# Two-layer attention kernel: the next batch's input and left operand fetched as 4 KB rows, three of seven operand parts fetched later

## The chip, the cores and the metric

One core of a Trainium2 chip runs the whole program. The metric is device time in microseconds (us) of one execution; the median of repeated runs is compared. Engines are named as in the profile: PE (TensorE matmul), PEld (its weight loads), DVE (VectorE), ACT (ScalarE), POOL (GpSimd), SP (SyncE, which here only issues DMAs). SPq is SP's instruction queue.

## The reference

Input x is (8, 512, 32, 32) float32: eight batches b, C = 512 channels, T = 1024 tokens. Two residual layers run in sequence, each on a group-normalised input:

```
x = x + layer0(gn(x))
x = x + layer1(gn(x))

layer 0: group norm again, q,k,v = qkv_w . n, 8 heads of 64, softmax(q k) v,
         out = proj_w . (xf + a) + proj_b
layer 1: q = w_q . x, k = w_k . x, v = w_v . x          (8 heads of 64)
         attn = einsum('bhqd,bhdT->bhqT', q, k) * scale
         attn = einsum('gh,bhqT->bgqT', w_head, attn)   # heads are mixed
         attn = softmax(attn), then instance norm over each (b, head)
         out  = attn v, then w_proj, + b_proj
```

The change touches layer 1 alone.

## The kernel before

**Stages.** Layer 0 runs over the eight batches first and writes its result to DRAM tensors `x1_d[b]`. Layer 1 then runs over the eight batches (loop L1930). For a batch it has three tensors in SBUF: `q`, `k` and `v`, each 128 partitions wide. The attention of a batch (class `Attention1`, L1620) is cut into eight tiles p of 128 queries, and the order of instructions on every engine is written out by hand, in `step(p, t, ag)` (L1854) with p from 0 to 8 and t from 0 to 3. Four sub-steps t make one step p; a step works on tile p (scores), on tile p-1 (head mixing and exponentials) and on tile p-2 (products with v). An `Agenda` object holds extra work by slot number 4p + t; `ag.at(slot, fn)` adds a function to a slot and `step` runs it there.

**The path of one tile.** `scores` (L1628) multiplies q and k for all eight heads, for 512 keys at a time (kh = 0 or 1), and ACT copies the result from PSUM to a `raw` tile (128 x 8 x 512; two buffers in all, so one for each kh). The head mixing needs the heads on different partitions. So `regroup` (L1649) moves the raw tile through the DMA engines: for each of four slices s and two halves r one DMA from 16 source partitions to a slot of `re`, 128 partitions x 512 floats, 256 KB. This makes 16 DMAs or 4 MB per step, all issued by SP (L1653). `mix` (L1663, matmul L1672) multiplies a slot of `re` by `wmix`; it needs both key halves of its slice. The first mix of tile p, `mix(p, 0)`, is issued in step p + 1 at t = 0, after the scores 0 to 2 and part of the value products.

**The order on SP's queue.** In each step SP issues six regroups (kh 0, s = 0, 1, 2) at t = 1, two more (kh 0, s = 3) at t = 2, then the prefetch pieces of that step if there are any (`self.piece`, L1918 and L1919), and at t = 3 the eight regroups of kh 1. A DMA waits on the completion of the DMA eight places earlier on the queue, because eight semaphores are used in turn.

**The prefetch.** During the attention of batch b the operands of batch b + 1 are loaded. `a.pieces` (L1942 and L1943) is a list of 30 DMAs of 128 KB, each 128 partitions x 256 floats (1 KB): sixteen of `y_piece` (L1337), which fill the next normalised input `y` (4 channel blocks of 128 x 1024) from `x1_d`, and fourteen of `left_piece` (L1302), which fill the next left operand for k. Four are issued in each of the steps 1 to 4, five in steps 5 and 6 and four in step 7. So steps 1 to 4 carry y and steps 5 to 7 carry the left operand. In the last batch (L1964) there is no next batch; eight pieces of w_proj (`p_piece`, L1327) are issued in steps 1 and 2, four in each, and nothing later.

**The left operand.** Projections use a scheme of seven products on 2 x 2 blocks (class `Projection`, L1363). The left operand has seven parts, each 128 x 512 floats. Product m reads the part given in `products` (L1374):

```
1: (0, self.b11), 2: (1, self.b21), 3: (6, self.b22), 4: (2, self.t[:, 3]),
5: (3, self.t[:, 0]), 6: (4, self.t[:, 1]), 7: (5, self.t[:, 2]),
```

**The tail.** Step 8 has no scores; it is called the tail below, with what follows it. There the k projection of batch b + 1 is woven in: products 1, 2, 6, 7 at slots 4 NT - 0.5, + 0.5, + 1.5 and + 2.5 (NT = 8), product 5 after `a.sums(last)` (L1981), products 4 and 3 later still (L1990). At slot 4 NT + 1 `left_p` (L1426) loads the 1792 KB left operand of the output projection into a raw buffer; SP then issues the next wv (L1325), the reciprocals of the last tile (L1779, L1786), the residual rows (L1515), the left operand for q (L1317) and the outputs (L1535).

Of the kernel before, what the change touches and what calls it, by code (L numbers as in the profile page):

```python
# [18 lines left out]
P = 128  # L19
# [448 lines left out]
def tile_two_attention_layers(  # L468
# [19 lines left out]
    nc = tc.nc  # L488
    B, C, T = x_d.shape
    H = w_head.shape[0]  # L490
    D = C // H
    NCC = C // P
    NT = T // P
# [9 lines left out]
    x1_d = [dram.tile([C, T], F32, tag=f"x1_{b}", name=f"x1_{b}") for b in range(B)]  # L503
# [193 lines left out]
    with ExitStack() as l0:  # L697
# [21 lines left out]
        for c in range(NCC):  # L719
# [5 lines left out]
        HC = C // 2  # L725
# [4 lines left out]
        left_d = {  # L730
            which: dram.tile([P, 7 * 2 * HC], F32, tag=f"left_{which}", name=f"left_{which}")
            for which in SOURCES
        }
        left_t = {}

        def left_tile(which, b):
            t = wpool.tile([P, 7, 2, HC], F32, tag="left", name=f"left_{which}_{b}")
            left_t[which] = t
            return t
# [463 lines left out]
        for b in range(B):  # L1203
            more = b + 1 < B
            ag = Agenda()
# [61 lines left out]
    with ExitStack() as l1:  # L1267
# [21 lines left out]
        y_t, qo_t, k_t, v_t = ({0: t["1"]} for t in (n_t, q_t, k_t, v_t))  # L1289
        w_t = {}  # L1290
# [3 lines left out]
        HC = C // 2  # L1294
# [4 lines left out]
                [P, 7, 2 * HC], F32, tag="left", name=f"left_{key[0]}_{key[1]}"  # L1299
            )  # L1300

        def left_piece(key, i):  # L1302

            if i == 0:
                left_tile(key)
            f, h = i // 2, i % 2
            return nc.sync.dma_start(
                out=w_t[key][:, f, ts(h, HC)],
                in_=left_d[key[0] + "1"][:, (2 * f + h) * HC : (2 * f + h + 1) * HC],
            )  # L1310

        def load_left(key, t=None):
# [11 lines left out]
            for c in range(NCC):  # L1324
                nc.sync.dma_start(out=w_t[key][:, c], in_=src[ts(c, P)])  # L1325

        def p_piece(i):  # L1327

            if i == 0:
                left_tile(("p", B - 1))  # L1330
                w_t["p", B - 1] = w_t["p", B - 1][:, :NCC]
            c, h = i // 2, i % 2
            return nc.sync.dma_start(
                out=w_t["p", B - 1][:, c, ts(h, HC)], in_=w_projT[ts(c, P), ts(h, HC)]
            )

        def y_piece(b, i):  # L1337

            if i == 0:
                y_t[b] = shared.tile([P, NCC, T], F32, tag="n", name=f"y_{b}")  # L1340
            c, r = i // 4, i % 4
            return nc.sync.dma_start(
                out=y_t[b][:, c, ts(r, HC)], in_=x1_d[b][ts(c, P), ts(r, HC)]
            )

        def normalize1(b, c):
            normalize_to(y_t[b][:, c], b, c)
# [272 lines left out]
        class Attention1:  # L1620
# [233 lines left out]
            def step(self, p, t, ag):  # L1854

                new, old, older = p < NT, p >= 1, p >= 2
                if t == 0:
                    if new:
                        for i in range(3):
                            self.scores(p, i)  # L1860
                    if older:
                        self.values(p - 2, 0, 2, 3)
                        self.leave(p - 2, 0)
                        self.sums(p - 2)
                        if p % 2 == 0 and p >= 4:
                            self.divide(p // 2 - 2, nc.gpsimd)
                    if old:
                        self.mix(p - 1, 0)()
                    ag.run(4 * p - 0.5)
                elif t == 1:  # L1870
                    if older:
                        self.values(p - 2, 1, 0)
                        self.flip(p - 1, 0)
                        self.totals(p - 2)
                        self.moments(p - 1, 0)
                    if new:
                        self.scores(p, 3)
                    if old:
                        self.mix(p - 1, 1)()
                    ag.run(4 * p + 0.5)  # L1880
                elif t == 2:
                    if older:
                        self.values(p - 2, 1, 1)
                    if new:
                        self.scores(p, 4)
                        self.scores(p, 5)
                    if old and not new:
                        self.mix(p - 1, 2)()
                    ag.run(4 * p + 1.5)
                    if older:  # L1890
                        self.values(p - 2, 1, 2, 3)
                        self.leave(p - 2, 1)
                    if old and new:
                        self.mix(p - 1, 2)()
                else:
                    if new:
                        self.scores(p, 6)
                        if old:
                            self.values(p - 1, 0, 0)
                            second = self.mix(p - 1, 3)  # L1900
                        self.scores(p, 7)
                        if old:
                            second()
                            self.values(p - 1, 0, 1)
                    else:
                        self.mix(p - 1, 3)()
                        self.values(p - 1, 0, 0, 1)
                    ag.run(4 * p + 2.5)
                k_leave()
                if p == 1 or old and t:  # L1910
                    self.flip(p - 1, t)
                    self.moments(p - 1, t)
                if new:
                    for kh, s in (
                        (), ((0, 0), (0, 1), (0, 2)), ((0, 3),), ((1, 0), (1, 1), (1, 2), (1, 3)),
                    )[t]:
                        self.regroup(p, kh, s)
                if old and t == 2:  # L1918
                    self.piece(4 if p < 5 else 5)  # L1919
                ag.run(4 * p + t)  # L1920

        def load_wv(b):
# [7 lines left out]
        for b in range(B):  # L1930
            more = b + 1 < B
            a = Attention1(b)
            ag = Agenda()
            for i in range(NV):
                ag.at(1 + 2 * i, lambda i=i: v_pair(b, NV + i))
            if b == 0:
                stages = group_stages(B - 1, B, small_psum1)
                for i in range(3):
                    ag.at(i, stages[i])
                ag.at(3, v_sums)  # L1940
            if more:
                a.pieces += [lambda i=i: y_piece(b + 1, i) for i in range(4 * NCC)]  # L1942
                a.pieces += [lambda i=i: left_piece(("k", b + 1), i) for i in range(14)]  # L1943
                for c in range(NCC):
                    ag.at(20 + c, lambda c=c: normalize1(b + 1, c))

                def k_go(*ms):
                    if not kp:
                        kp.append(k_projection(b + 1))
                    for m in ms:  # L1950
                        kp[0].products(m)
                        due.append(lambda m=m: kp[0].leave(m))

                kp = []
                ag.at(4 * NT - 0.5, lambda: right_tile(b + 1))
                ag.at(4 * NT - 0.5, lambda: k_go(1))
                ag.at(4 * NT, lambda: right_y(b + 1, [0, 1]))
                ag.at(4 * NT + 0.5, lambda: k_go(2))
                ag.at(4 * NT + 1, lambda: right_y(b + 1, [2, 3]))
                ag.at(4 * NT + 1, lambda: left_p(b))  # L1960
                ag.at(4 * NT + 1.5, lambda: k_go(6))
                ag.at(4 * NT + 2.5, lambda: k_go(7))
            else:
                a.pieces += [lambda i=i: p_piece(i) for i in range(2 * NCC)]  # L1964
            for p in range(NT + 1):
                for t in range(4):
                    a.step(p, t, ag)
            ag.flush()
            k_leave()
            last = NT - 1  # L1970
            a.sums(last)
            if not more:
                a.values(last, 0, 2, 3)
                a.leave(last, 0)
                a.values(last, 1, 0, 1, 2, 3)
                a.leave(last, 1)
                a.totals(last)
                a.instance()
                out1_last(a)
                continue  # L1980
            k_go(5)  # L1981
            a.values(last, 0, 2, 3)
            a.leave(last, 0)
            load_wv(b + 1)
            a.values(last, 1, 0, 1, 2, 3)
            a.leave(last, 1)
            a.totals(last)
            a.instance()
            k_leave()
            k_go(4, 3)  # L1990
            k_leave()
            a.instance_end()
            v_pair(b + 1, 0)
            a.divide(NCH - 1)
            for g in range(H):
                a.affine(g)
            right_o = re_t[:, 4:8]
            combine_right(right_o, out_view(b))
            op = out1(b, right_o)
            load_left(("q", b + 1))  # L2000
            v_pair(b + 1, 1)
            a.check()
            op.run()
            q_projection(b + 1).run()
# [70 lines left out]
```

## Time and profile before

| what | value |
|---|---|
| runs shown | 4078.61, 4088.58, 4091.99 us; median 4088.58 |
| profiled execution, its own time | 4076.99 us |
| span of its profile | 4075.2 us |
| mean granted PE clock | 0.991 |
| busy share of the span | PE 96%, PEld 45%, DVE 70%, ACT 48%, POOL 3% |
| layer 1 | from 1800 us on, eight batches |
| DMA share in layer 1 | 0.61 to 0.69 of 16 engines by stages of 275 to 400 us, 0.23 to 0.25 in layer 0 |
| regroup DMAs | 1024, 256 KB each |
| y pieces, left pieces | 112 and 98, 128 KB each |

The page gives busy time by engine, then 40 slices of the span, the DMA queues, and groups of instructions by source line with the idle time ahead of them and what ended it. A timeline row is: start, duration, engine, line, operation, output <- inputs, count, and in brackets the idle time before it and what released it. A windows row gives, for a stretch, the engines' busy time, the granted PE clock as a share of full speed, the busy share of the DMA engines and the GB/s that they moved. Busy shares of DMA can exceed 1, because the records of packets overlap.

### The profile page before, as it was taken

Reading aid. Unit: us, or ns where it says so; the run is one execution under the profiler, and the core shown is the slowest. Engines: PE = TensorE matmul, PEld = TensorE weight load, DVE = VectorE, ACT = ScalarE, POOL = GpSimd, SP = SyncE. Lnnn points to the kernel's source line nnn. Section 1 sums busy time; section 2 is a strip of 40 time slices with the busy share of each in tenths; the row PEclk is TensorE's granted clock in tenths of the full one; section 3 lists DMA queues with packets and bytes.
Section 4 is the critical chain, followed back from the end, with each engine's and each line's share of the span. In section 5 each row is a group of like instructions: output and inputs, shape, how many; then the busy total and the mean of one; then the engine's idle time right before and its main releaser. Section 6 shows DMA issues by size and latency. Waiting matters only on the chain. (4 is left out here: it accounts for less than half of the span.)

```text
span 4075.2 us, 96122 instructions
## 1 busy us (share of the span) xinstructions
PE 3906.7 (96%) x41932; PEld 1839.3 (45%) x41932; DVE 2835.6 (70%) x4124; ACT 1967.2 (48%) x2431; POOL 128.6 (3%) x150
## 2 busy tenths in 40 slices
PE   8999999999999999999999999999999999999997
PEld 4353535353434434344535545445444444445354
DVE  4748474757666665748859859759679578488597
ACT  1717263635445453517427437347157175174274
POOL 0000000000000000000000000001000000000000
PEclk9999999999999999999999999999999999999999
DMA  3313131212112111238639549468378287386384
GB/s 127 109 47 115 50 115 45 89 47 79 46 60 71 65 54 59 74 104 213 172 118 226 173 123 228 136 154 224 119 183 224 84 217 184 114 214 180 115 214 126
DMA packets 268637, 519.13 MB, mean 127 GB/s; under 512 B 49840, under 2 KB 84912, under 8 KB 261552
## 3 DMA queue, kind: packets, MB, share of 16 engines
q1 hardware_dynamic: 261664, 497.96, 42.8%
q0 software_dynamic: 6544, 14.94, 1.7%
q8 instruction: 332, 5.44, 0.6%
q14 instruction: 97, 0.79, 0.1%
HBM read 197.16 MB, written 46.92 MB: 60 GB/s over the span
## 5 line engine op out<-in xcount | busy, mean ns | idle before, releaser
L1700 DVE STREAM_TRANSPOSE et<-e 128x2048 f32<-128x2048 f32 x256 | 587.3, 2294 | 153.4 <-ACT e L1685 146.8
L1727 PEld LDWEIGHTS a<-et,v 128*64 128x64 f32 x16384 | 514.3, 140 | 296.7 <-issue 226.9
L1711 DVE BATCH_NORM_STATS2 bn<-e 128x6 f32<-128x512 f32 x1024 | 633.9, 674 | 0.0
L1685 ACT ACTIVATE e<-m 128x1024 f32<-128x1024 f32 x512 | 502.9, 1023 | 237.5 <-issue 134.1
L1089 ACT ACTIVATE e<-s 128x1024 f32<-128x1024 f32 x512 | 497.2, 1026 | 233.8 <-PE s L1084 232.7
L1727 PE MATMUL a<-et,v 128*64 128x64 f32 x16384 | 562.8, 226 | 11.0 <-DVE et L1700 10.4
L1647 ACT COPY raw<-s 128x1024 f32<-128x1024 f32 x480 | 469.8, 1017 | 195.8 <-PE s L1635 165.9
L1097 DVE TENSOR_TENSOR zacc<-zacc,e 128x1024 f32<-128x1024 f32 x384 | 468.7, 1221 | 91.0 <-ACT e L1089 69.0
L1635 PE MATMUL s<-k,q 64*64 64x512 f32 x4096 | 515.9, 607 | 6.2 <-DVE q L1500 3.1
L1084 PE MATMUL s<-q,k 64*64 64x512 f32 x4096 | 490.1, 593 | 2.3 <-ACT e L1089 2.3
L1110 PE MATMUL a<-e,v 64*64 64x512 f32 x4096 | 484.1, 589 | 0.0
L1672 PE MATMUL m<-re,wmix 32*32 32x512 f32 x8192 | 329.3, 617 | 104.7 <-DMA re<-raw 54.7
L1110 PEld LDWEIGHTS a<-e,v 64*64 64x64 f32 x4096 | 156.7, 133 | 282.8 <-issue 282.2
L1084 PEld LDWEIGHTS s<-q,k 64*64 64x64 f32 x4096 | 147.9, 133 | 275.1 <-issue 240.5
L1635 PEld LDWEIGHTS s<-k,q 64*64 64x64 f32 x4096 | 128.4, 132 | 262.5 <-issue 93.6
L1461 PE MATMUL pv<-wv,y 128*128 128x512 f32 x480 | 212.1, 597 | 0.0
L1743 ACT COPY q<-a 64x256 f32<-64x256 f32 x256 | 93.9, 367 | 180.8 <-PE a L1727 178.8
L1672 PEld LDWEIGHTS m<-re,wmix 32*32 32x32 f32 x8192 | 73.6, 103 | 196.6 <-issue 77.8
L1779 POOL DMA_DIRECT2D zd<-rz x56 | 34.6, 619 | 3514.0 <-DVE r L1791 3514.0
L1461 PEld LDWEIGHTS pv<-wv,y 128*128 128x128 f32 x480 | 89.3, 190 | 116.9 <-issue 110.3
L1465 ACT COPY v<-pv 128x512 f32<-128x512 f32 x30 | 17.6, 586 | 218.6 <-PE pv L1461 218.6
L1095 DVE TENSOR_TENSOR zacc<-e,e 128x1024 f32<-128x1024 f32 x64 | 78.3, 1223 | 57.2 <-ACT e L1089 57.2
(315 smaller groups left out, 3951.2 us busy)
## 6 DMA issues: line engine op xcount, KB each, us to landing
re<-raw SPq DMA_DIRECT2D x1024, 256.0 KB
left_q<-left_q SPq DMA_DIRECT2D x17, 1792.0 KB
left_p<-left_p SPq DMA_DIRECT2D x17, 1792.0 KB
left_k<-left_k SPq DMA_DIRECT2D x10, 1792.0 KB
x<-in_x_dram SPq DMA_DIRECT2D x32, 512.0 KB
rzb<-zd SPq DMA_DIRECT2D x128, 128.0 KB
x<-x SPq DMA_DIRECT2D x64, 256.0 KB
left_v<-left_v SPq DMA_DIRECT2D x8, 1792.0 KB
```

The lines of the kernel that those rows point to most:

```text
L1084: nc.tensor.matmul(ps[c * D : c * D + D, m], k[r, hp, k0 : k0 + D], q[r, hp, ts(f, FB)], start=True, stop=True,)
L1089: nc.scalar.activation(e[i], ps, AF.Exp, scale=S0 * S0)
L1097: nc.vector.tensor_add(zacc[g], zacc[g], e[i])
L1110: nc.tensor.matmul(acc[g][a][m * D : m * D + D], v[rows, kc, ts(2 * hp + m, D)], e[i][rows, m], start=(kc == 0), stop=(kc == NG - 1),)
L1461: nc.tensor.matmul(ps[:, m], y_t[b][:, c, ts(2 * i + m, P)], w[:, c], start=(c == 0), stop=(c == NCC - 1),)
L1635: nc.tensor.matmul(ps[c * D : c * D + D, m], qo_t[b][r, p, hp, ts(c, D)], k_t[b][r, hp, ts(kh, FB)], start=True, stop=True,)
L1647: nc.scalar.copy(dst, ps)
L1672: nc.tensor.matmul(ps[a // 2][c * 32 : c * 32 + 32, a % 2].rearrange("p (r h k) -> p h r k", r=2, h=2), wmix[rows].rearrange("p g i -> p ( ...
L1685: nc.scalar.activation(e[:, :, 2 * h : 2 * h + 2].rearrange("p r a k -> p a r k"), ps[h].rearrange("p a (r k) -> p a r k", r=2), AF.Exp,)
L1700: nc.vector.transpose(self.et[p, u].rearrange("p kb (r st a) g q -> p st kb r (a g q)", r=2, st=2)[:, st], self.e[p, s].rearrange("p r a ( ...
L1711: nc.vector.bn_stats(self.bn[p][:, s, a], e[:, :, a].rearrange("p r k -> p k r"))
L1727: nc.tensor.matmul(acc[two * D : two * D + D, s].rearrange("p (x q) -> p x q", q=4), v_t[b][:, kb, ts(g, D)], et[:, kb, :, g], start=(kb = ...
```

## The change

The 30 pieces per batch become eight DMAs. `y_piece` loads one channel block of 128 x 1024 floats (512 KB, 4 KB on each partition) in one DMA. `left_piece(key, f, n)` loads n whole parts in one DMA (4 KB on each partition for n = 2). `self.piece()` issues one entry of the list in each step, so steps 1 to 4 carry one y block each, step 5 the parts 0 and 1, step 6 the parts 4 and 5. The parts 2 and 3 (512 KB) and 6 (256 KB) leave the list; they are put on the agenda at slot 4 NT, at the end of t = 0 of step 8, ahead of `right_y` and of `left_p`. In the last batch `p_piece` loads one block of 256 KB (2 KB on each partition) in each of the steps 1 to 4.

```diff
-        def left_piece(key, i):
+        def left_piece(key, f, n):
-            if i == 0:
+            if f == 0:
                 left_tile(key)
-            f, h = i // 2, i % 2
-            return nc.sync.dma_start(
-                out=w_t[key][:, f, ts(h, HC)],
-                in_=left_d[key[0] + "1"][:, (2 * f + h) * HC : (2 * f + h + 1) * HC],
+            nc.sync.dma_start(
+                out=w_t[key][:, f : f + n].rearrange("p f o -> p (f o)"),
+                in_=left_d[key[0] + "1"][:, 2 * f * HC : 2 * (f + n) * HC],
             )
...
-        def p_piece(i):
+        def p_piece(c):
-            if i == 0:
+            if c == 0:
                 left_tile(("p", B - 1))
                 w_t["p", B - 1] = w_t["p", B - 1][:, :NCC]
-            c, h = i // 2, i % 2
-            return nc.sync.dma_start(
-                out=w_t["p", B - 1][:, c, ts(h, HC)], in_=w_projT[ts(c, P), ts(h, HC)]
-            )
+            nc.sync.dma_start(out=w_t["p", B - 1][:, c], in_=w_projT[ts(c, P)])
-        def y_piece(b, i):
+        def y_piece(b, c):
-            if i == 0:
+            if c == 0:
                 y_t[b] = shared.tile([P, NCC, T], F32, tag="n", name=f"y_{b}")
-            c, r = i // 4, i % 4
-            return nc.sync.dma_start(
-                out=y_t[b][:, c, ts(r, HC)], in_=x1_d[b][ts(c, P), ts(r, HC)]
-            )
+            nc.sync.dma_start(out=y_t[b][:, c], in_=x1_d[b][ts(c, P), :])
...
                 if old and t == 2:
-                    self.piece(4 if p < 5 else 5)
+                    self.piece()
...
-                a.pieces += [lambda i=i: y_piece(b + 1, i) for i in range(4 * NCC)]
-                a.pieces += [lambda i=i: left_piece(("k", b + 1), i) for i in range(14)]
+                a.pieces += [lambda c=c: y_piece(b + 1, c) for c in range(NCC)]
+                a.pieces += [lambda f=f: left_piece(("k", b + 1), f, 2) for f in (0, 4)]
+                ag.at(4 * NT, lambda: left_piece(("k", b + 1), 2, 2))
+                ag.at(4 * NT, lambda: left_piece(("k", b + 1), 6, 1))
...
-                a.pieces += [lambda i=i: p_piece(i) for i in range(2 * NCC)]
+                a.pieces += [lambda c=c: p_piece(c) for c in range(NCC)]
```

## Prediction

> **What bounds the kernel now.** PE is busy 96% of the span, so only idle PE time can be won, or PE time at a reduced clock. I read in this order: the page's slices, the group of the mix matmul, PE's waits over batches 1 to 6, then the timelines of PE and of SP's queue, and the clock in windows.
>
> ```profile
> DMA  3313131212112111238639549468378287386384
> ...
> L1672 PE MATMUL m<-re,wmix 32*32 32x512 f32 x8192 | 329.3, 617 | 104.7 <-DMA re<-raw 54.7
> ```
>
> The second half of the slices (layer 1) has busy DMA engines, and of all PE groups the mix has by far the most idle time ahead of it. PE's waits, 2100 to 3850 us (total, times, longest):
>
> ```profile
> PE m L1672 <- DMA re<-raw: 40.9, 21, 4.5
> PE m L1672 <- issue: 22.0, 8, 4.8
> PE m L1672 <- ACT q L1743: 18.3, 12, 2.3
> ```
>
> PE waits for regrouped scores. "issue" and "ACT q" are mostly the same wait under another name: the waiting instruction is the first mix of a step too. PE's timeline of batch 1 (steps 5, 6, 7, tail; x24 scores open a step):
>
> ```profile
> 2207.38 2.81 PE L1635 MATMUL s<-k,q 64*64 64x512 f32 x24
> 2213.54 1.15 PE L1672 MATMUL m<-re,wmix 32*32 32x512 f32 x32 [1.34 <-issue]
> ...
> 2229.49 2.81 PE L1635 MATMUL s<-k,q 64*64 64x512 f32 x24
> 2236.28 1.27 PE L1672 MATMUL m<-re,wmix 32*32 32x512 f32 x32 [1.97 <-DMA re<-raw]
> ...
> 2253.75 2.81 PE L1635 MATMUL s<-k,q 64*64 64x512 f32 x24
> ...
> 2281.85 2.02 PE L1672 MATMUL m<-re,wmix 32*32 32x512 f32 x32 [4.55 <-DMA re<-raw]
> ```
>
> The same in batch 7, steps 6 and 7 and tail, where no pieces are issued after step 2:
>
> ```profile
> 3957.68 2.81 PE L1635 MATMUL s<-k,q 64*64 64x512 f32 x24
> ...
> 3979.15 2.81 PE L1635 MATMUL s<-k,q 64*64 64x512 f32 x24
> 3983.90 1.14 PE L1672 MATMUL m<-re,wmix 32*32 32x512 f32 x32
> ...
> 4005.23 2.02 PE L1672 MATMUL m<-re,wmix 32*32 32x512 f32 x32 [2.52 <-DMA re<-raw]
> ```
>
> Batch 7 is an experiment made already: a step without pieces ahead takes 3979.15 - 3957.68 = 21.47 us (steps 4, 5, 6: 21.36, 21.57, 21.47). From the same score rows of batches 0 to 6, a step behind a y piece takes 22.39 (mean of 28) and step 6, behind five left pieces, 24.04 (mean of 7). In the tail PE waits 4.22 us for its first mix (mean of 7) and 2.52 in batch 7. The SP queue shows where the pieces stand:
>
> ```profile
> 2203.44 2.44 SPq L1342 DMA_DIRECT2D y<-x  x4
> 2207.48 18.03 SPq L1653 DMA_DIRECT2D re<-raw  x16
> ...
> 2271.53 3.54 SPq L1307 DMA_DIRECT2D left_k<-left_k  x4
> 2275.46 6.91 SPq L1653 DMA_DIRECT2D re<-raw  x8
> ```
>
> They stand just ahead of the kh 1 regroups that the next mix waits for: 2207.48 to 2213.54 is 6.1 us, 2275.46 to 2281.85 is 6.4 us. The DMA engines have a share of about 1.0 there. The clock after the 1.97 us wait:
>
> ```profile
> 2236.00:2237.00 1.00, 0.72 (x32) 1.00 1.05 279
> 2237.00:2238.00 1.00, 1.00 (x28) 0.60 1.06 279
> 2238.00:2239.00 1.00, 1.00 (x24) 0.50 1.05 274
> ```
>
> PE's clock falls to half for 3.4 us. The clock records of the trace hold 19 such stretches, all in layer 1: in step 6 of batches 0, 1, 2, 5, 6; in step 7 of batches 0, 3, 5; in the tail of all eight (one of double length); one in step 2 of batch 0; two more in the last 50 us.
>
> [...] in step 4 of batch 1 the 1 KB packets run through between 2184 and 2187.5, and the kh 1 packets mostly follow them. [...] The packet records show more: in layer 0 a 1 KB packet takes 46 ns and a 4 KB packet (x loads) 159 (medians), so 184 against 159, 14%. The measured ratio is used. [...] The trace has stretches of 3413 ns at 0.5, after waits of only 2.0 to 2.5 us; shorter waits than 1.9 led to none in a step.
>
> **The change part by part.** Sums are made against the profiled execution (4077.0, span 4075.2), which lies 11.6 below the median of the runs.
>
> *y pieces, steps 1 to 4.* Same bytes, same place. In layer 1 the 1 KB packets take 64 ns on average (packet records). A piece is 8 packets per engine, 0.52 us; four make 2.06. One 4 KB row by the ratio 159/46: 223 ns, 8 of them 1.78 us. Gain 0.28 per step. Bounds: nothing, if under contention time goes by bytes (4 KB packets of the rzb broadcast take 245 ns here: 1.96, gain 0.10), and 0.8 at best (4 x 0.52 - 8 x 0.159). The waits there average 1.37 us and can fall by 0.9 before the 21.4 us of a clean step is reached, so 0.28 counts fully: 28 x 0.28 = 8 us.
>
> *Left parts, steps 5 and 6.* Five pieces (2.58 us) become one of 1.78. So step 6 should become as long as a y step after the change, 22.39 - 0.28 = 22.1, instead of 24.04: the wait is 0.8 shorter, and falls below the 1.9 that led to half clock. 7 x 1.9 = 13 us. Step 7 waits 2.04 now (mean), three times with half clock: 0.8, plus 3/7 of about 1.5; 1.4, minus what the ACT wait at 0.85 in batch 1 won't give back: 1.3. 7 x 1.3 = 9 us.
>
> *No piece in step 7.* The wait for `mix(7, 0)` goes to batch 7's 2.52: 1.70 x 7 = 12. The half clock came in batch 7 too, so I count it gone in one tail or two only: 2. Together 14. What is late next is the regroup itself: 4.4 us from the last raw copy's end (4000.84) to the mix with an empty queue.
>
> *The moved parts in the tail.* Two DMAs of 768 KB in all, at 260 GB/s 3 us, queued on SP behind the last regroups and ahead of `left_p`, so nothing that mixes need is behind them. They land near 2290 on batch 1's clock. Product 5, which now carries a wait on them, starts near 2308.4 (half of the x16 products at 2304.87, 7.13 us long); products 4 and 3 at 2321. Cover 18 us; queued behind product 5 on PE are the values of the last tile, so a loss of the cover would cost its lateness one for one. `left_p` (1792 KB) moves back by at most 3 us of DMA; SP's next DMA, wv, is issued at 2314, and the windows 2294 to 2314 have DMA almost idle. POOL's zd and rzb transfers share the engines for that time, and `divide` uses them only 25 us later. Counted as 0; range 0 to 2 us in all.
>
> *Fewer issues.* 22 fewer DMA issues per batch on SP, at 0.65 us each. Mostly SP would have waited for the raw copy anyway (pieces end 2205.88, copy 2207.45). In step 6 the five pieces last until 2254.78 and the copy ended at 2253.82: about 1 us late, contained in the 9 above.
>
> *Last batch.* The same 1 MB of pieces over four steps instead of two: 1 us less in steps 2 and 3, about as much more in 4 and 5. 0, between -2 and +2.
>
> Sum: 8 + 13 + 9 + 14 = 44 us. From the median: 4088.6 - 44 = 4045; from the profiled execution 4033.
>
> **Rivals.** (B) Bytes decide: the 4 KB rows gain nothing in y steps, and the half clock stays in half of the steps. For it: the regroups move at 264 GB/s and 1 KB pieces at about 240, so little is left. Then 28 x 0 + 7 x 1.0 + 7 x 0.6 + 12 = 23, 4065. (C) The waits sit on an edge, and y steps come down to 21.6, step 6 too, with half clock gone from most tails: 28 x 0.8 + 7 x 2.4 + 7 x 1.7 + 7 x 2.5 = 69, 4020. For it: batch 7's steps; against: 1.78 of 2.06 us of pieces remain. (D) Nothing measurable: the regroup's own latency takes over (the tail's 2.5 us stays, and other steps find the DVE or ACT wait instead, as in batch 7's z1 waits of 0.7); 4082. (E) Slower: the 4 KB rows from HBM hold the engines longer. Place: the ring ahead of the kh 1 regroups in steps 1 to 6. The price is 28 x (8t - 2.06) + 14 x (8t - 2.58) - 12 for a packet time t; it turns to a loss from t = 0.315 us. For it: rzb packets of 4 KB in mixed stretches take 270 to 370 ns; against: those all read the same rows, and x loads take 187 on average. At t = 0.40 it gives +29: 4117.
>
> **How the numbers follow.** The forecast (A) has 0.58, B 0.19, C 0.12, D 0.06, E 0.05. About 12 us, 0.3%, is what a measurement can tell from no change. A, C and nearly all of B are faster by more: 0.58 + 0.12 + 0.17 = 0.87. The rest of B, D and a fifth of E (a small loss) lie within it: 0.02 + 0.06 + 0.01 = 0.09. E leaves 0.04. The range takes in B's and C's times and A's open terms: 4018 to 4074.
>
> **What would show it.** In the profile after: mix waits on DMA in the tail of 2.5 us instead of 4.2; steps 2 to 5 near 22.1; step 6 near 22.1 rather than 24.0; half-clock stretches down from 19 to about 9; 4 KB packets near 220 ns; no PE wait ahead of product 5. Packets above 300 ns, a wait on left_k at product 5, or step 6 still at 24 would make the prediction wrong.

## The result and the profile after

| kernel | median of its runs, us | range, us | ratio to before, 95% interval |
|---|---|---|---|
| before, same chip | 4085.34 | 4078.61 to 4091.99 | |
| changed | 4051.94 | 4047.25 to 4056.02 | 0.9918 [0.9897, 0.9939] |
| changed, run again beside before at 4090.50 | 4054.15 | 4051.90 to 4056.95 | 0.9912 [0.9897, 0.9928] |

The median of before is 4085.34 here and not 4088.58, because a fourth run, 4082.10, counts with the three shown. The change gains 33 and 36 us; 44 were predicted. The direction and the mechanism hold, and the sum was 8 to 11 us too large. The profiled execution took 4047.25 (span 4045.5); against that of before the spans differ by 29.7 us, because the profile of before was a low draw, 8 to 12 us under the medians.

The page of the changed kernel has the same shape as before; two of its lines moved, the mix group and the packets of SP's queue:

```profile
q1 hardware_dynamic: 238912, 497.95, 42.9%
...
L1665 PE MATMUL m<-re,wmix 32*32 32x512 f32 x8192 | 322.7, 605 | 81.4 <-DMA re<-raw 67.8
```

The same megabytes go in 22,752 fewer packets, and the share of the DMA engines stays at 42.9% (42.8% before, of a span 0.7% longer): what the larger packets saved of the transfers is too little to be seen in the sum. The mix group lost 23.3 us of idle time (104.7 before) and 6.6 us of busy time: the same 8192 matmuls at 605 instead of 617 ns, as fewer of them run at half clock (12 stretches instead of 19, table below). Together that is 29.9 us, about the difference of the spans. PE's waits in layer 1 of the changed kernel (total us, times, longest us), 2095 to 3830 us:

```profile
PE m L1665 <- DMA re<-raw: 51.0, 32, 2.8
PE m L1665 <- ACT q L1736: 9.8, 8, 1.9
...
PE m L1665 <- issue: 0.4, 1, 0.4
```

The three names under which the mix waits sum to 61.2 us, and to 81.2 before. The longest fell from 4.8 to 2.8. Batch 1 on PE's timeline, steps 5, 6, 7 and tail:

```profile
2204.91 2.81 PE L1628 MATMUL s<-k,q 64*64 64x512 f32 x24
2211.34 1.15 PE L1665 MATMUL m<-re,wmix 32*32 32x512 f32 x32 [1.61 <-DMA re<-raw]
...
2228.55 2.81 PE L1628 MATMUL s<-k,q 64*64 64x512 f32 x24
2233.72 1.15 PE L1665 MATMUL m<-re,wmix 32*32 32x512 f32 x32 [0.35 <-issue]
...
2250.44 2.81 PE L1628 MATMUL s<-k,q 64*64 64x512 f32 x24
...
2277.65 2.02 PE L1665 MATMUL m<-re,wmix 32*32 32x512 f32 x32 [2.56 <-DMA re<-raw]
```

The tail's wait is 2.56 (4.55 before), as in batch 7 before the change; the wait of a y step, 1.61, is not shorter than the 1.34 before. SP's queue over the same time, and the tail on PE:

```profile
2200.99 0.77 SPq L1337 DMA_DIRECT2D y<-x  x1
2205.01 20.46 SPq L1646 DMA_DIRECT2D re<-raw  x16
...
2250.54 29.42 SPq L1646 DMA_DIRECT2D re<-raw  x24
2280.00 1.46 SPq L1306 DMA_DIRECT2D left_k<-left_k  x2
2284.00 0.32 SPq L1316 DMA_DIRECT2D left_p<-left_p  x1
```

```profile
2298.60 2.08 PE L1720 MATMUL a<-et,v 128*64 128x64 f32 x64
2300.61 7.13 PE L1379 MATMUL pk<-right,left_k 128*128 128x512 f32 x16
2307.68 5.82 PE L1720 MATMUL a<-et,v 128*64 128x64 f32 x192
```

The y block is one issue ahead of the regroups, nothing stands ahead of the tail's regroups, and the two moved DMAs come after the last of them. The x16 row holds products 7 and 5; no wait in brackets stands before it, nor before any other product of the k projection in the layer, so the moved parts cost PE nothing.

A table by steps, from the score rows of the timelines (batches 0 to 6, mean us), with the number of half-clock stretches in the clock records of the trace, and the mean clock over each kernel's runs:

| kernel | y steps 2 to 5 | step 6 | step 7 and tail | half-clock stretches | clock of runs |
|---|---|---|---|---|---|
| before | 22.39 | 24.04 | 135.7 | 19 | 0.988 to 0.989 |
| changed | 22.43 | 23.0 | 132.3 | 12 | 0.993 |
| changed, again | 22.55 | 22.87 | 132.4 | 12 | 0.993 |

In the changed kernel the stretches are in the tails of batches 0, 1, 2, 5, 6 and 7, in step 6 of batches 0 and 6, in one y step and one step 1, and two at the end. The one in step 1 of batch 0 has no PE wait ahead of it; why it is there is open. Before to after, over seven batches: y steps +1.2 us, step 6 -7.3, step 7 and tail -23.7, batch 7 -0.8; with +1.3 in step 1 of batch 0 and -0.4 ahead of layer 1 that is the 29.7. Step sums of a single profile move by some 10 us from one execution to the next with the number of half-clock draws, so rows are read together with the runs. What a step from 3 to 6 is made of comes out of the same timelines: about 20.9 us, plus the waits of PE in it, plus half the time of its half-clock stretches. In the changed kernel the first mix of a y step waits 1.28 us on average, and that of step 6 1.43; before it was 1.39 and 1.99.

### The profile page after: what moved, and what is told of

Same layout as the page of the kernel before. It is cut to its first block, busy times and chain, and to the rows that moved or that the text cites. A ratio compares the mean times of both kernels' runs of the same rounds, so it can differ in the third digit from the quotient of the medians.

```text
span 4045.5 us, 95879 instructions
## 1 busy us (share of the span) xinstructions
PE 3895.9 (96%) x41932; PEld 1835.3 (45%) x41932; DVE 2833.2 (70%) x4124; ACT 1966.6 (49%) x2431; POOL 128.5 (3%) x150
## 3 DMA queue, kind: packets, MB, share of 16 engines
q1 hardware_dynamic: 238912, 497.95, 42.9%
## 5 line engine op out<-in xcount | busy, mean ns | idle before, releaser
L1693 DVE STREAM_TRANSPOSE et<-e 128x2048 f32<-128x2048 f32 x256 | 587.4, 2294 | 137.1 <-ACT e L1678 131.8
```

What stands on the lines that cost most here:

```text
L1693: nc.vector.transpose(self.et[p, u].rearrange("p kb (r st a) g q -> p st kb r (a g q)", r=2, st=2)[:, st], self.e[p, s].rearrange("p r a ( ...
```

## The experiments

The theory after the result (called the place theory here): what costs is that a piece stands on SP's queue just ahead of the kh 1 regroups that PE's next mix waits for; the change gains where it takes bytes from that place (step 7 and the tail, a part of step 6), and little or nothing by the shape of the packets. Rivals: the shape of the packets brings a large part; the bytes as such, wherever they stand, load the engines; the moved parts or other bounds (DVE, the regroup's own latency) take back what was won. Each experiment says which kernel it changes, and ratios are to the kernel before on the same chip.

**Shape alone** (on the changed kernel: parts 2, 3 and 6 back in step 7).

```diff
-                ag.at(4 * NT, lambda: left_piece(("k", b + 1), 2, 2))
-                ag.at(4 * NT, lambda: left_piece(("k", b + 1), 6, 1))
+                a.pieces += [lambda: (left_piece(("k", b + 1), 2, 2), left_piece(("k", b + 1), 6, 1))]
```

> The 4 KB rows alone: the pieces as in the changed kernel, but all seven parts of the left operand in steps 5 to 7 (parts 0 and 1, parts 4 and 5, then 2, 3 and 6 in step 7), nothing in the tail. Theory 1 (bytes ahead of the kh 1 regroups decide, not their shape): steps 5 and 6 carry 512 KB instead of 640 and gain about 7 us in all, step 7 carries 768 KB instead of 512 and loses about 1 us in each of 7 tails; y steps unchanged. Total about 4085, ratio 1.000 (0.997 to 1.002). Theory 2 (fewer issues and longer rows decide): most of the gain of the change is here, 4055 to 4065, ratio 0.993 to 0.995.

Measured: 4077.14, ratio 0.9975 [0.9961, 0.9988]. About 10 us of the gain. But the shape isn't all that differs from the kernel before: steps 5 and 6 carry 512 KB each where they carried 640, and step 7 carries 768 KB where it carried 512.

**Move alone** (on the kernel before: the six pieces of parts 2, 3 and 6, in 1 KB rows, to slot 4 NT).

```diff
-                    self.piece(4 if p < 5 else 5)
+                    self.piece(4)
...
-                a.pieces += [lambda i=i: left_piece(("k", b + 1), i) for i in range(14)]
+                a.pieces += [lambda i=i: left_piece(("k", b + 1), i) for i in (0, 1, 2, 3, 8, 9, 10, 11)]
+                for i in (4, 5, 6, 7, 12, 13):
+                    ag.at(4 * NT, lambda i=i: left_piece(("k", b + 1), i))
```

> The move alone: the pieces of 128 KB with 1 KB rows as before, four in each of the steps 1 to 6 (left parts 0 and 1 in step 5, 4 and 5 in step 6), and the six pieces of parts 2, 3 and 6 in the tail at slot 4 NT. Theory 1: all of the gain is here, tails shorter by 3.4 us each as in the changed kernel, step 6 by about 1; about 4052, ratio 0.992. Theory 2: tails gain, but steps do not; 4065 to 4070, ratio 0.995 to 0.996.

Measured: 4065.19, ratio 0.9942 [0.9927, 0.9957]. About 24 us. The two ratios multiply to 0.9975 x 0.9942 = 0.9917, the ratio of the whole, but that doesn't show two independent parts. Here too steps 5 and 6 carry 512 KB instead of 640, so both runs hold that cut: step 6 fell from 24.04 to 22.74 here and to 22.60 with the shape alone, in 1 KB rows as in 4 KB rows, and in the whole it counts once. Step 7 and tail tell the two apart: they fell from 135.7 to 133.2 here, and rose to 137.1 with the shape alone.

**The piece behind the regroups** (on the changed kernel: the same DMAs, bytes and packets, one stage later, after the regroup loop).

```diff
-                if old and t == 2:
+                if old and t == 3:
```

> The changed kernel with each piece issued at t = 3 behind the kh 1 regroups instead of at t = 2 ahead of them. Theory 1: the first mix of the next step no longer waits behind the piece; the steps behind a y block go from 22.4 to 21.5 us (28 x 0.9 = 25), steps 6 and 7 gain 0.9 each (13): about 4015, ratio 0.983. Rival (the regroups alone keep the wait, or the kh 0 regroups and the raw copies, now behind the piece, are late by as much): about 4050, ratio 0.992.

Measured: 4020.10, ratio 0.9829 [0.9813, 0.9844]: 32 us faster than the changed kernel by the medians, 34 to 36 by the ratios, with the same bytes in every step. SP's queue and PE's timeline in a y step of batch 1:

```profile
2139.56 18.24 SPq L1646 DMA_DIRECT2D re<-raw  x16
2157.85 1.41 SPq L1337 DMA_DIRECT2D y<-x  x1
```

```profile
2150.96 2.81 PE L1628 MATMUL s<-k,q 64*64 64x512 f32 x24
2155.71 1.14 PE L1665 MATMUL m<-re,wmix 32*32 32x512 f32 x32
...
2171.92 2.81 PE L1628 MATMUL s<-k,q 64*64 64x512 f32 x24
```

The mix starts 4.75 us after the scores without a wait, and the step takes 20.96 us; the mean of the y steps falls from 22.4 to 21.65, and the wait of their first mix from 1.28 to 0.27. "Bytes as such" falls: the bytes are the same. Step 6 does not follow: 22.7, though no piece is ahead of its mix any more and that mix waits only 0.32. Something else holds it here (below).

**The old pieces behind the regroups** (on the kernel before, the same edit: 1 KB rows, 30 issues, four or five pieces a step, nothing moved to the tail).

> The kernel before with one edit: its pieces (1 KB rows, 4, 5 or 4 a step, all parts in steps 5 to 7) are issued at t = 3 behind the kh 1 regroups. If the place of the pieces on SP's queue is what costs, and neither their rows nor the number of issues, this gives what the changed kernel gave and more: y steps at 21.5, step 7's pieces behind the regroups that the tail waits for; 4020 to 4028, ratio 0.983 to 0.985. If 1 KB rows or 22 more issues cost by themselves: 4045 or more, 0.989.

Measured: 4025.83, ratio 0.9849 [0.9825, 0.9873]. With the place mended, shape, number of issues and the move together are worth no more than the difference to the experiment above, 0.9829 against 0.9849, whose intervals overlap. The move was one way out of the bad place, and this is another.

**Each y block twice** (on the changed kernel; the second copy goes to a spare buffer).

```diff
+            if c == 0:
+                left_tile(("spare", b))
+            f = 2 * (c % 3)
+            nc.sync.dma_start(
+                out=w_t["spare", b][:, f : f + 2].rearrange("p f o -> p (f o)"),
+                in_=x1_d[b][ts(c, P), :],
+            )
```

> The changed kernel with each y block loaded twice, the second time to the left operand's buffer, which is unused in those steps; so 1 MB instead of 512 KB stands ahead of the kh 1 regroups in steps 1 to 4. The second copy is not used. Theory 1: each of the 28 steps behind it grows by the DMA time of 512 KB, 1.9 us, more where the clock halves: 4100 to 4120, ratio 1.004 to 1.008. Rival (the waits of the y steps have another cause): under 10 us more than the changed kernel, 4052 to 4062.

Measured: 4118.26, ratio 1.0077 [1.0063, 1.0090]: 66 us slower than the changed kernel. Its y steps take 25.0 instead of 22.43, 71.9 us over the 28 of them, or 2.57 us for each extra 512 KB ahead of the regroups. Two y steps of its batch 1 on PE's timeline:

```profile
2164.31 2.81 PE L1635 MATMUL s<-k,q 64*64 64x512 f32 x24
2172.13 2.10 PE L1672 MATMUL m<-re,wmix 32*32 32x512 f32 x32 [3.00 <-DMA re<-raw]
...
2190.78 2.81 PE L1635 MATMUL s<-k,q 64*64 64x512 f32 x24
2200.17 2.02 PE L1672 MATMUL m<-re,wmix 32*32 32x512 f32 x32 [4.57 <-DMA re<-raw]
```

The wait grows, from 1.28 to 3.08 us on average of the 28 steps, and the x32 row itself takes 2.0 to 2.1 us instead of 1.15, the length that this row has at half clock (2.02 us at a granted clock of 0.50 in the tail of batch 1 of the changed kernel). The 1.80 us that the wait grows by are about the DMA time of a block (8 packets per engine; 1.86 us at the 232 ns of the changed kernel, 1.63 at the 203 of this run). The step pays more, 2.57: these steps hold 22 units of 3.4 us at half clock, against 1 in the changed kernel.

**The y pieces as 1 KB rows again, single and double** (on the changed kernel, and on the one with each block twice: four DMAs for each block).

```diff
-            nc.sync.dma_start(out=y_t[b][:, c], in_=x1_d[b][ts(c, P), :])
+            for r in range(4):
+                nc.sync.dma_start(out=y_t[b][:, c, ts(r, HC)], in_=x1_d[b][ts(c, P), ts(r, HC)])
```

> The changed kernel with the y blocks alone in four DMAs of 1 KB rows as before; left operand and tail as changed. The prediction's step for y (0.28 us in each of 28 steps) expects 8 us more than the changed kernel, 4060. The packet records of the changed kernel (4 KB packets 236 ns, so 1.89 us for a block instead of 2.06) expect 28 x 0.17 = 5 us, 4057. If bytes alone decide: no difference, 4052.

> As y_double (each y block fetched twice, the second time to the unused left buffer), but both in 1 KB rows, eight DMAs a step. Against y_double (ratio 1.0077), which moves the same bytes in 4 KB rows: by the prediction's 0.28 us per block 56 x 0.28 = 16 us more, 1.0116; by the packet records 56 x 0.17 = 10 us more, 1.010; if bytes alone decide 1.0077. If the number of issues on SP matters by itself (six more in each of 28 steps, 0.65 us each), far more: over 1.02.

Measured: single 4058.65, 0.9923 [0.9910, 0.9937], beside the changed kernel's 4054.15, 0.9912 [0.9897, 0.9928] on the same chip. Double 4124.71, 1.0079 [1.0063, 1.0094], against 1.0077 [1.0063, 1.0090] for 4 KB rows, taken on another chip. The single pair differs by 4.5 us with overlapping intervals, the double pair not at all. The shape of the y rows is worth 0 to 5 us; that it is above zero is not resolved. (For the expectation's 236 ns the trace of the changed kernel gives 232, so 0.2 us per block where it has 0.17.)

**The unchanged kernel again**, beside the 1 KB kernels.

> The changed kernel itself, unaltered, on the same chip as the three that follow, so that they can be compared with it. 4052, ratio 0.992.

Measured: 4054.15, 0.9912 [0.9897, 0.9928], as in the first table.

**Behind, and product 1 ahead of the tail's first mix** (on the kernel with the piece behind the regroups).

```diff
+                    if not new:
+                        ag.run(4 * p - 0.5)
                     if old:
                         self.mix(p - 1, 0)()
```

> The kernel with the pieces behind the kh 1 regroups, and in the tail product 1 of the k projection (4 us on PE) issued ahead of the first mix instead of after it. Theory: what stays of the tail's wait, 2.5 us, is the regroup's own latency with an empty queue, and half clock follows from it; work that doesn't depend on it hides both: 7 x 2.5 + 7 x 0.7 x 1.7 = 26 us less than 4020, so about 3995, ratio 0.977. Rival: the exponentials that follow the first mix become late by the 4 us of the product, and PE waits for ACT instead: 4015 to 4025, 0.982 to 0.985.

Measured: 3992.38, ratio 0.9760 [0.9746, 0.9775]. The tail on PE's timeline:

```profile
2256.12 3.70 PE L1379 MATMUL pk<-y,left_k 128*128 128x512 f32 x8
2259.76 1.14 PE L1665 MATMUL m<-re,wmix 32*32 32x512 f32 x32
```

The mix has no wait, and its x32 row takes 1.14 us. In the changed kernel it waits 2.56 us and then runs 2.02 us at a granted clock of 0.50. The regroup's own latency, which the move leaves in the tail, is filled with 3.7 us of work that needs no regroup. Step 7 and tail take 128.3 instead of the 131.9 of the kernel with the piece behind. Six half-clock stretches of 19 are left, and the mean clock of the runs is 0.996.

**What holds step 6: block 2's normalisation one slot earlier, block 1's one later** (on the changed kernel).

```diff
-                for c in range(NCC):
-                    ag.at(20 + c, lambda c=c: normalize1(b + 1, c))
+                for c, slot in ((0, 20), (2, 21), (1, 22), (3, 23)):
+                    ag.at(slot, lambda c=c: normalize1(b + 1, c))
```

> The changed kernel with the second of the two y blocks that DVE normalises taken one sub-step earlier (block 2 at slot 21, block 1, which ACT does, at 22). The question is why step 6 fell from 24.0 to 22.9 us and not to the predicted 22.1. Theory: DVE's normalisation at the start of step 6 stands still while GpSimd's divide runs (its duration is the overlap plus 0.55 us), which delays DVE's chain and PE's z product; taken earlier it does not meet the divide, step 6 comes to about 22.2 (5 us in 7 steps) and half clock there goes: 4046, ratio 0.990. Rival (the piece ahead of the regroups alone sets step 6): 4052, ratio 0.992, step 6 at 22.9.

The reason to try it is this stretch of batch 1 of the kernel with the piece behind the regroups, at the start of step 6 (all engines):

```profile
2217.07 2.95 DVE L692 TENSOR_SCALAR y<-y,gmean,grstd 128x1024 f32<-128x1024 f32 x1
2217.09 2.37 POOL L1811 TENSOR_TENSOR q<-q,rzb 128x1024 f32<-128x1024 f32 x1 [5.66 <-DMA rzb<-zd]
...
2225.53 0.39 PE L1757 MATMUL z<-sel,zz 128*64 128x32 f32 x4 [2.09 <-DVE zz L1750]
```

DVE normalises block 2 while POOL divides, in the same 2.4 us. The normalisation takes 2.95 us, DVE's chain is late by that, and PE waits 2.09 us for zz. The same line over the whole trace, min/median/max in ns, in that kernel and in the experiment:

```profile
L692 DVE TENSOR_SCALAR y<-y,gmean,grstd x16: 783/808/2954, 1682.6 to 3623.2; 128x1024 f32<-128x1024 f32 x16
```

```profile
L692 DVE TENSOR_SCALAR y<-y,gmean,grstd x16: 783/804/810, 1682.7 to 3659.7; 128x1024 f32<-128x1024 f32 x16
```

Measured: 4047.74, ratio 0.9903 [0.9883, 0.9923]. The long normalisation is gone, and step 6 falls from 23.0 and 22.9 to 21.35. That the normalisation held it does not follow, for the edit moves a second thing: block 1, which ACT normalises in 1.24 us, comes later on ACT and stands ahead of a copy of raw scores near the end of step 5. PE's score matmuls wait for that copy; batch 1 of the experiment:

```profile
2226.50 1.24 ACT L688 ACTIVATE y<-y,gneg,grstd 128x1024 f32<-128x1024 f32 x1
2228.70 1.09 PE L1628 MATMUL s<-k,q 64*64 64x512 f32 x8 [0.89 <-ACT raw L1640]
```

This wait of 0.89 us is in step 5 of all seven batches, and in none of the changed kernel. It comes behind the issue of the piece and ahead of the kh 1 regroups, so the piece has a longer lead: it is issued 4.74 us ahead of the scores of step 6 instead of 3.54 or 3.59 (means of seven batches). The wait of step 6's first mix falls from 1.43 and 1.28 us to 0.18, and the two half-clock stretches that step 6 has in the first profile of the changed kernel are gone; the wait for zz was 0.18 and 0.48, and is 0.26. What left step 6 of the changed kernel is thus mostly the known wait, and a part of it only moved into step 5, which rises from 22.7 or 22.8 to 23.3. The profiled execution was the slowest of the six, 4060.83, and its y steps are long as a whole (22.94 on average). The time, 0.9903 against 0.9918 and 0.9912, does not resolve a gain.

**The same on the fastest kernel.**

> The kernel with pieces behind the regroups and product 1 ahead of the tail's first mix, with the same earlier normalisation. There step 6 has no piece ahead of its regroups and still took 22.7 to 23.3 us. Theory as above: step 6 comes to 21.6, 7 x 1.2 = 8 to 12 us less: 3982, ratio 0.9735. Rival: DVE, busy 19 us of a step, has no room in step 5 and gives the time back there: 3990, ratio 0.976.

Measured: 3988.68, ratio 0.9761 [0.9739, 0.9783], against 0.9760 [0.9746, 0.9775] without it. Step 6 falls from 23.35 to 21.39, step 5 rises from 21.26 to 22.08; 7 x (1.96 - 0.82) = 8 us by the profiles, and the ratios show none of it, though their intervals leave room for as much. Here, where the mix of step 6 hardly waits with or without the edit (0.07 and 0.00 us), it is DVE that holds step 6: the wait for zz falls from 1.40 to 0.20 us, and of the seven batches without the edit the three with a normalisation of 1.8 to 2.6 us have the step 6 of 24.5 to 26.0 us, the others 21.7 to 22.4. Step 5 pays the 0.89 us for ACT's copy again, nearly all that it rises by. Block 2 alone, with block 1 left in its slot, was not tried.

## Why the prediction was right, and where it was not

**The bound**, the first mix of a step waiting for regroups that stand behind pieces on SP's queue: shown. Moving the piece behind them, with nothing else changed, makes the changed kernel 32 to 36 us faster, and the kernel before, with its 1 KB rows, 62 to 64.

**Step 7 and tail** (predicted 9 + 14 = 23 us): 23.7 in the first profile of the changed kernel and 22.7 in the second. The tail's wait went from 4.22 to 2.72 on average (2.52 predicted), step 7's from 2.04 to 1.33 (a fall of 0.7; 0.8 predicted). The move alone gained about 24 us in all, 17 of them in step 7 and tail by its profile. The remaining 2.5 us of the tail were rightly named as the regroup's own latency; the swap of product 1 showed that they could be hidden.

**The moved parts at no cost**: right. No PE wait stands before product 5.

**The y pieces** (predicted 28 x 0.28 = 8 us): mis-sized. The 4 KB packets of the prefetch take 232 ns on average in layer 1 (228 in the second profile), where 223 was taken from the ratio 159/46 of two medians in the quiet layer 0. Transfers add up, so the mean is the measure: the means there are 187 and 52 ns, and their ratio would have given 64.8 x 187/52 = 233. So 8 x 232 = 1.86 us against 2.07 leave 0.2 per step, 6 us (7 in the second profile), and the saving is 10 to 12%, not 14%. The 1 KB experiments show 0 to 5 us, and the y steps of the profile none (22.39 before, 22.43 and 22.55 after).

**Step 6** (predicted 7 x 1.9 = 13 us): this step failed. I expected that it "should become as long as a y step after the change", since only the pieces seemed to set it apart from one, and that its half clock would go. It fell to 23.0 and 22.9, 7 to 8 us in all. The y steps stayed at 22.4 and 22.6 themselves, not 22.1. The wait of step 6's first mix fell from 1.99 to 1.43 and 1.28, by 0.6 to 0.7 where 0.8 was expected. The rest differs between the two profiles: in the first, two of the seven steps kept their half clock; in the second none did, but PE waited 0.48 us for zz (0.15 before). That is a second bound, which I had not looked for: DVE's normalisation meets POOL's division there. The trace of before showed it already, with normalisations of 1.23 to 1.67 us in five of the seven steps instead of 0.8. It holds step 6 once no piece is ahead of the mix (1.05 us for zz in the step of 22.7).

**The sum**: 0 to 5 for the y steps, 7 to 8 for step 6 and 23 to 24 for step 7 and tail make 30 to 37 us, where 33 and 36 were measured. The 8 to 11 us that are missing from 44 are these two terms.

**Half clock**: from 19 stretches to about 9 predicted, 12 measured. It went from two of the eight tails (one or two were counted), and from step 7 altogether, but stayed twice in step 6 (in the second profile once in step 7, and not in step 6). The clock difference of the runs, 0.0045 to 0.005, is worth at most 18 to 20 us of PE time (4060 us x 0.005), so somewhat more than half of the gain at most can be clock; it is an upper bound, since a part of a stretch can lie under a wait (the one in the tail of batch 1 begins at 2277.26, 0.39 us before the end of the wait at 2277.65).

**Fewer issues** and **the last batch** (0 each): six more issues in each of 28 steps changed nothing (each y block twice, 1.0079 against 1.0077), and the kernel that keeps all 30 but has them behind the regroups leaves little for them; batch 7 changed by 0.8 us, within the -2 to +2.

**Rivals.** E (the 4 KB rows hold the engines, loss from 315 ns): refuted, 232 and 228 ns. B (bytes decide, 4065) was nearer than the forecast in the y steps (0) and in step 6 (7 us), and wrong in step 7 and tail, where it gave 16 us (7 x 0.6 + 12) and 23 to 24 were measured. C (y steps down to 21.6): not with the piece ahead of the regroups; the y steps stayed at 22.4. With the piece behind them they take 21.65, and the kernel 4020.10. D (nothing measurable) is excluded by both intervals.

**The best version** is the piece behind the regroups with product 1 ahead of the tail's first mix: 3992.38 beside 4054.15 for the changed kernel on the same chip, whose runs (3990.18 to 3998.82 and 4051.90 to 4056.95) are far apart.

## What to carry to other kernels

On a queue that serves both prefetches and transfers that the compute engine waits for, look first at the order: moving the prefetch behind the urgent transfer won more here (0.985 with the old shape) than shaping and partly moving it (0.992). What still waits for a transfer's own latency can be covered by independent work placed ahead of the waiting instruction (0.976 here, from 0.983). When a step is expected to become like its neighbours, look through all engines at its start for what else only it carries. When an experiment swaps two pieces of work, follow both: here the one that was not meant made most of the difference.

## What the runs showed of the hardware

- **DVE and POOL at the same time.** The 128x1024 tensor_scalar takes 0.80 to 0.82 us alone (before and changed), and 2.95 us (the kernel with the piece behind), 2.25 (changed, batch 6), 1.67 and 1.42 (before, batches 3 and 1) when it overlaps POOL's tensor_tensor for 2.37, 1.70, 1.12 and 0.86 us: the overlap plus 0.55 to 0.58 us each time. So about 0.25 us of its 0.80 are done during an overlap of 0.86 us as of 2.37 (an estimate from these spans; POOL's in the trace are rough). Where DVE started 0.57 us ahead, in batch 0 of the kernel before, with an overlap of 0.21, it is POOL's row that is longer: DVE took 0.783 us and POOL 2.45, where its median is 2.36. In the case of 2.95 it is DVE's row that starts first too, but by 0.02 us only. Why the two hold each other up was not shown.
- **Half clock after short waits.** In the profile of the kernel before no PE wait of up to 1.86 us in layer 1 has a stretch of 3.4 us at 0.5 behind it; of those from 1.95 to 2.35 us six have one and seven have not, and all longer ones have. These traces give no sharp limit: in the changed kernel a wait of 2.84 us has none. A second y block ahead of the regroups, 1.80 us more wait, cost 2.57 us per step with the half clock that came of it.
- **Packets quiet and under load.** On average 52 ns (1 KB) and 187 ns (4 KB) in the quiet layer, 65 and 232 or 228 ns in the busy one: both grow by about a quarter, and the larger packet saves 10 to 12% in either. The medians, 46 and 159 against 59 and 224, would make it 14% and 5%.
